# Moving a conditioned layer from blocks of 512 tokens behind a planned stage into that stage, sample by sample

## The chip, the cores and the metric

The kernel runs on one core of a Trainium2 chip. It uses five engines: TensorE (PE), which multiplies matrices; VectorE (DVE), ScalarE (ACT) and GpSimd (POOL), which work element by element; and SyncE (SP), which issues most of the transfers. Each engine runs its own list of instructions in order and waits on semaphores for the others. The metric is the device time of one launch, in microseconds (us), as the median of several runs. Everything is computed in float32.

## The reference

The input x holds 16 samples of 256 tokens with 256 features. Four residual steps follow one another. The change concerns the conditioned layer inside the last of them:

```python
# 1: x += attention0(cross_attention(x, side))                 16 heads of 16
# 2: x += fp4_feed_forward(x @ W[cat[b]] + b[cat[b]])          quantized in blocks of 16
# 3: x += segment_attention(reaction_diffusion(x, zX, zY, zR)) 16 heads of 64, segments of 128, 16 memory tokens
# 4:
h = gelu(x @ fc1_w.T + fc1_b)                   # 256 -> 1024, the erf form
shared = h @ fc2_w.T + fc2_b                    # 1024 -> 192
own = h @ experts_w[idx[b]].T + experts_b[idx[b]]   # 1024 -> 64, one of 16 experts per sample
y = concat(shared, own)                         # 256 features again
x += SCALE * (shared_expert(y) + sum(gate_e * expert_e(y) for the best 2 of 8 experts))
```

An expert of the mixture is 256 -> 1024, gelu (the tanh form), 1024 -> 256. The expert of the conditioned layer ("own") is chosen by the sample, those of the mixture by the token.

## The kernel before, in words

**Two parts.** `woven` (L329) does steps 1 to 3 for all samples; `mixture` (L1286) does step 4.

**The woven part** is written as 18 generators, one for each stage. stage_a, stage_m, stage_x and stage_e are step 1 (projections, scores, exponentials b_e, values and output projection); stage_y and stage_f are step 2 (the layer by category, then the quantized feed-forward with its tiles d_h, q_xn, q_big); stage_gate, stage_up and stage_down prepare its weights once; stage_d is the reaction-diffusion of step 3 (e_u, e_zT); stage_p, stage_k and stage_u make queries, keys and values of a group of four heads (weights wq and wv, rotated tiles f_t1q, f_t2q, f_t1k, f_t2k, which are moved into f_q and keys by transfers); stage_s, stage_g and stage_v do scores, exponentials (f_prob) and values with the output projection (f_pT, f_oT, wo, added to x); stage_c is described below; stage_fill gives PE idle products until the first sample is under way. There are 64 head groups in step 3, four for each sample.

**The planner.** `weave` (L201) merges the generators into one list of instructions for each engine, when the program is built. It keeps a model of when each engine is free and each tile is written and read (costs in L118 to L124). In each round it takes from every stage its next operation, works out at what time that could start, and issues the one that can start first; on a tie the stage that stands first in one list of stages, the same for all engines. An operation can have two choices of engine: `copy_` (L323) is a copy on ACT or DVE. Tiles live in rings of a fixed number of buffers; a new tile waits until the oldest buffer's readers are done. The order found is the order on the chip: an engine that waits for one operand lets nothing pass. Matmul results of the woven part go into PSUM tiles named `single` (four, one bank each) and `pair` (two, two banks each).

**Between the parts.** After step 1 of the last sample the memory of its tiles is given up, and `fetch_c` (L489) loads into it the first two samples of x from DRAM (`xd`, written by stage_v after step 3 of each sample) and the weights of the conditioned layer: fc1, fc2, wr (the router's weights), and two tiles own0 and own1, whose first 64 columns are shared and whose last 64 are a sample's own expert. `stage_c` (L518) then computes the first layer of block 0 (512 tokens, the hidden tile hT0) as the last stage of the woven part.

**The mixture part** is scheduled in program order. `conditioned` (L1594) loops over 8 blocks of 512 tokens: it loads own weights and later samples of x, transposes x (g_xT or xT), adds the shared expert's bias bs2 to x on POOL, computes 8 groups of 128 hidden columns of fc1 with a Gelu each, the 128 shared outputs with fc2, the 64 shared and 64 own outputs of each sample (yT), and the router's products (wr). `route` (L1463) chooses the experts and their ranks on DVE and sends each row of y to its two places in `ysort` by 8 indirect scatters per block from POOL (L1513). `plan_tiles` (L1521) then lays out the expert tiles, four shared blocks (`shared_block`, L1340, 512 tokens of the shared expert each) follow, then 35 expert tiles of 256 rows (`expert_tiles`, L1388), each of which loads its rows ys from `ysort` and its two weight matrices, then the other four shared blocks with `combine` (L1412), which gathers each token's two expert rows and stores the output.

The rule by which the planner chooses, and its costs:

```python
COSTS = {"DVE": (0.15, 0.00105), "ACT": (0.16, 0.00083), "POOL": (0.30, 0.0016)}
...
                found.append([start + (GAP if op.filler else 0.0), rank, c[1], w, c, start, part])
        if found:
            x = min(found, key=lambda x: x[:3])
            best = (x[:3], x[3], x[4], x[5])
```

Of the kernel before, what the change touches and what calls it, by code (L numbers as in the profile page):

```python
# [19 lines left out]
P = 128  # L20
# [42 lines left out]
def setup(ctx, tc, a, n_batch):  # L63
# [22 lines left out]

    k.xd = [dram.tile([S, D], F32, name=f"xd{b}") for b in range(n_batch)]
# [36 lines left out]
GAP = 0.6  # L124

# [9 lines left out]
def rows_of(op):  # L135

    if len(op.ins) < 2 or op.ins[0].shape[0] > 64:
        return None
    first, n = op.ins[0].start_partition() // 32, 1 + (op.ins[0].shape[0] > 32)
    return range(first, first + n), 0.15 + row_size(op.ins[1]) * 0.00178  # L140
# [17 lines left out]
class Unit:  # L158
# [5 lines left out]
    def __getattr__(self, fn):  # L164
        call = getattr(self.engine, fn)

        def make(*args, **kw):
            aps = [x for x in args if is_ap(x)] + [v for n, v in kw.items() if is_ap(v) and n not in ("out", "accum_out")]
            outs = [kw[n] for n in ("out", "accum_out") if n in kw and is_ap(kw[n])]
            if "out" not in kw:  # L170
                outs.insert(0, aps.pop(0))
            return Op([(self.name, self.cost(fn, outs, aps), lambda: call(*args, **kw))], outs, aps)  # L172

        return make
# [26 lines left out]
def weave(streams):  # L201
# [58 lines left out]
    waiting = [[s, None, None] for s in streams]  # L260
    while waiting:
        best, moved, found = None, False, []
        for rank, w in enumerate(waiting):
# [15 lines left out]
            for c in op.choices:  # L279
# [7 lines left out]
                found.append([start + (GAP if op.filler else 0.0), rank, c[1], w, c, start, part])  # L287
# [40 lines left out]

def woven(k):  # L329
    nc, tc = k.nc, k.tc  # L330
    with ExitStack() as ctx:
# [18 lines left out]
        g.x, g.io, g.done = {}, {}, {"J": 0, "T": 0, "K": 0, "X": 0, "S": 0, "VT": 0, "U": 0, "Y": 0, "H": 0, "W": 0, "D": 0, "Z": 0, "A": 0, "M": 0, "E": 0, "F": 0, "P": 0, "G": 0, "V": 0, "L": 0, "R": 0, "C": 0}  # L350
        with tc.manual_schedule():
            weave([stage_f(g), stage_a(g), stage_m(g), stage_x(g), stage_e(g), stage_v(g), stage_y(g), stage_d(g), stage_s(g), stage_g(g), stage_p(g), stage_k(g), stage_u(g), stage_gate(g), stage_up(g), stage_down(g), stage_c(g), stage_fill(g)])
# [50 lines left out]
def stage_a(g):  # L403
# [17 lines left out]
    for b in range(g.B):  # L421
# [3 lines left out]
        if b + 1 < g.B:  # L425
            yield lambda: b + 1 < g.done["L"] + 5
            yield from fetch_a(g, b + 1)
# [19 lines left out]
def stage_m(g):  # L447

    g.shifted = {}
# [39 lines left out]
def fetch_c(g):  # L489
# [3 lines left out]
    hT0 = k.h0.__enter__().tile([P, 8, 512], F32, name="hT0")  # L493
    k.c2 = k.tc.tile_pool(name="c2_w", bufs=1, side="right")
    w = k.c2.__enter__()
    k.early = {"hT0": hT0}

    def get(name, shape, src=None):
        k.early[name] = t = w.tile(shape, F32, name=name)
        if src is not None:  # L500
            yield g.sp.dma_start(out=t, in_=src)

    yield from get("x0", [P, 4, D])
    for b in range(2):
        yield g.sp.dma_start(out=k.early["x0"][:, 2 * b : 2 * b + 2, :], in_=k.xd[b].rearrange("(s p) d -> p s d", p=P))
    yield from get("fc1", [P, 2, FF1], a["fc1"])
    yield from get("fc1b", [P, 8], a["fc1b"])
    yield from get("fc2", [P, 8, P], a["fc2a"])
    yield from get("wr", [P, 2, P + NE])
    yield g.sp.dma_start(out=k.early["wr"][:, :, P:], in_=a["w_router"])  # L510
    for i in range(2):
        yield from get(f"own{i}", [P, 8, P])
        yield g.sp.dma_start(out=k.early[f"own{i}"][:, :, 0:64], in_=a["fc2c"])
    yield from get("xT0", [P, 2, 512])
# [3 lines left out]
def stage_c(g):  # L518


    yield lambda: g.done["C"] and g.done["G"] == 4 * g.B
    e = g.k.early
    x, xT = e["x0"], e["xT0"]
    for c in range(2):
        one = yield from single(g, x)
        pt = one.rearrange("p (s t) -> p s t", t=P)
        for s in range(4):
            yield g.pe.transpose(pt[:, s, :], x[:, s, c * P : (c + 1) * P], g.ident)
        yield copy_(g, xT[:, c, :], one)
        g.singles.append(one)  # L530
    for f in range(8):
        one = yield from single(g, xT)
        yield from mm_(g, one, [(e["fc1"][:, c, f * P : (f + 1) * P], xT[:, c, :]) for c in range(2)])
        yield g.act.activation(e["hT0"][:, f, :], one, AF.Gelu, bias=e["fc1b"][:, f : f + 1])
        g.singles.append(one)
# [37 lines left out]
def cross_attention(g, b):  # L573
# [17 lines left out]
    for st in range(2):  # L591
        yield g.dve.tensor_scalar(e[:, st, :], e[:, st, :], stat[:, 2 + st : 3 + st], None, ALU.mult)
# [49 lines left out]
def heads_scores(g, i):  # L642
# [19 lines left out]
    for st in (1, 0):  # L662
        n = (st + 1) * P
        four = yield from quad(g, t, kd)
# [6 lines left out]
        for jp, two in enumerate(four):  # L671
            e = g.a_.tile([P, 4, n], F32, name=f"b_e{st}", tag=f"b_e{st}", bufs=3)
# [82 lines left out]
def stage_y(g):  # L755
# [5 lines left out]
    for b in range(g.B):  # L761
        yield lambda b=b: g.done["A"] > b
        if b + 1 < g.B:
            yield from fetch_f(g, b + 1)
        g.yT[b] = yield from conditioned_rows(g, b)
# [3 lines left out]
def fetch_f(g, b):  # L769
    wc = g.f_.tile([P, 2, D], F32, name="wc", tag="wc", bufs=2)  # L770
    bc = g.f_.tile([P, D], F32, name="bc", tag="bc", bufs=2)
# [50 lines left out]
def scratch_l(g, wide, narrow):  # L822

    tags = dict(q_xn=wide[0], q_big=wide[1])
    shape = {"f_pT": [P, 4, P], "f_prob": [P, 2, 4, PM + P], "wq": [P, 2, 2, 2 * P], "f_v": [P, 2, 4 * DH1]}
    bufs = {"f_pT": 3, "f_prob": 2, "wq": 2, "f_v": 3}
# [54 lines left out]
def stage_down(g):  # L881

    g.downT = g.w.tile([P, 6, D], F32, name="downT")
    scratch = scratch_l(g, ("f_prob", "wq"), "down")
# [82 lines left out]
def stage_p(g):  # L967
# [34 lines left out]
    pmv = tile_l(g, [P, 2, 2, 2 * P], "wq", 2)  # L1002
    yield g.sp.dma_start(out=pmv, in_=a["pmv"].rearrange("p c (r w) -> p c r w", r=2))
    for c in range(2):
        wo = tile_l(g, [P, 4, D], "wq", 2)
        yield g.sp.dma_start(out=wo, in_=a["w_out1"][:, 4 * c : 4 * c + 4, :])
# [3 lines left out]
        for i in range(4):  # L1010
            yield g.pe.transpose(pt[:, i, :], pmv[:, c, i // 2, (i % 2) * P : (i % 2 + 1) * P], g.ident)
        yield copy_(g, pmvT, pt)
        g.singles.append(one)
        one = yield from single(g, pmvT, wo)
# [18 lines left out]
    g.wq, g.queries = {0: (yield from fetch_p(g, 0))}, {}  # L1033
    for i in range(4 * g.B):
        yield lambda: g.done["D"] > i // 4 and i < g.done["S"] + 2 and g.done["K"] >= i
        if i + 1 < 4 * g.B:
            g.wq[i + 1] = yield from fetch_p(g, (i + 1) % 4)
        q = g.queries[i] = tile_l(g, [P, 2, S], "f_q", 2)
        move = lambda half, a, src: g.sp.dma_start(out=q[half, a, :], in_=src)
        yield from turned4(g, g.zT[i // 4], g.wq[i][:, 0], "q", DH1**-0.5, move)  # L1040
# [3 lines left out]
def stage_k(g):  # L1044

    yield lambda: g.done["Z"]
    by_seg = lambda t: t.rearrange("p (s t) -> p s t", s=2)
    for i in range(4 * g.B):
        yield lambda: g.done["D"] > i // 4 and i < g.done["S"] + 4 and i in g.wq
        keys = g.keys[i % 4]  # L1050
        move = lambda half, a, src: g.sp.dma_start(out=keys[half, a, :, PM:], in_=by_seg(src))
        yield from turned4(g, g.zT[i // 4], g.wq[i][:, 1], "k", None, move)
# [51 lines left out]
def fetch_p(g, n):  # L1104

    wq = tile_l(g, [P, 2, 2, 2 * P], "wq", 2)
    for which in range(2):
        cols = slice((8 * which + 2 * n) * P, (8 * which + 2 * n + 2) * P)
        yield g.sp.dma_start(out=wq[:, which], in_=g.a["w_qk1"][:, :, cols])
    return wq  # L1110


def stage_u(g):
# [3 lines left out]
    for i in range(4 * g.B):  # L1117
# [3 lines left out]
        v, before = tile_l(g, [P, 2, 4 * DH1], "f_v", 3), wv  # L1121
        if i + 1 < 4 * g.B:
            wv = yield from fetch_u(g, (i + 1) % 4)
        zT = g.zT[i // 4]
        one = yield from single(g, before, zT)
        pv = one.rearrange("p (s d) -> p s d", s=2)
        for st in range(2):
            yield from mm_(g, pv[:, st, :], [(zT[:, c, st * P : (st + 1) * P], before[:, c, :]) for c in range(2)])
# [6 lines left out]
def fetch_u(g, n):  # L1135

    wv = tile_l(g, [P, 2, 4 * DH1], "wv", 2)
# [4 lines left out]
def turned4(g, zT, w, name, scale, move):  # L1142

    one = yield from single(g, w, zT)
    pq = one.rearrange("p (r t) -> p r t", r=2)
    for r in range(2):
        yield from mm_(g, pq[:, r, :], [(w[:, c, r * P : (r + 1) * P], zT[:, c, :]) for c in range(2)])
    t1, t2 = tile_l(g, [P, 2, S], f"f_t1{name}"), tile_l(g, [P, 2, S], f"f_t2{name}")
# [9 lines left out]
    for a in range(2):  # L1158
        for r in range(2):
            yield move(slice(r, P, 2), a, t1[64 * a : 64 * a + 64, r, :])  # L1160

# [4 lines left out]
def stage_s(g):  # L1166

    g.scored = {}
# [13 lines left out]

def stage_v(g):

    for i in range(4 * g.B):
# [4 lines left out]
        if n == 3:  # L1190
            yield g.sp.dma_start(out=g.k.xd[b].rearrange("(p s) d -> p s d", p=P), in_=g.x.pop(b))
# [27 lines left out]
def exponentials4(g, n, prob, stat):  # L1219

    wo = tile_l(g, [P, 2, D], "wo", 2)
    yield g.sp.dma_start(out=wo, in_=g.a["w_out1"][:, 2 * n : 2 * n + 2, :])
# [12 lines left out]
    return prob, g.pm, wo  # L1235


def values4(g, n, b, v, prob, pm, wo):
# [20 lines left out]
    oT = tile_l(g, [P, 2, S], "f_oT", 2)  # L1259
# [13 lines left out]
    for st in range(2):  # L1273
# [4 lines left out]
        yield from mm_(g, pp[:, st, :], pairs)  # L1278
    yield g.dve.tensor_tensor(g.x[b], g.x[b], pp, ALU.add)
# [6 lines left out]
def mixture(k, out):  # L1286
# [5 lines left out]
    with ExitStack() as ctx:  # L1292
# [4 lines left out]
        for b in range(2):  # L1297
# [3 lines left out]
        k.yT = keep.tile([P, 2, B * S], F32, name="yT")  # L1301
        k.b1 = keep.tile([P, NE + 1, 8], F32, name="b1")
        k.bs2 = keep.tile([P, D], F32, name="bs2")
        nc.sync.dma_start(out=k.b1, in_=a["b1"])
        nc.sync.dma_start(out=k.bs2, in_=a["b2"][NE : NE + 1].to_broadcast([P, D]))
        nc.vector.tensor_scalar(k.bs2, k.bs2, OUT_SCALE, None, ALU.mult)
        r = routing_state(k, keep)
        w1s = keep.tile([P, 2, FF1], F32, name="w1s")
        w2s = keep.tile([P, 8, D], F32, name="w2s")
# [464 lines left out]
```

## Time and profile before

| | us |
|---|---|
| median of 3 runs | 2705.15 (2704.03 to 2711.97) |
| profiled execution | 2715.88 |
| its span | 2714.1 |
| busy: PE, DVE, ACT, POOL | 2582.5, 1456.7, 1086.8, 987.0 |
| first product of the mixture part's experts | 2099.4 |

The profile is of one execution. A group of instructions is written as line, engine, operation, tile written, tile read, shapes and count; most operations of the woven part have line L172, where a helper records them, so tiles tell them apart. Busy shares of a slice are in tenths (9 is 90% or more). PEclk is the share of full speed that PE's clock was granted. A matmul of float32 over 128 rows and 256 columns shows as two records, and the weights of a matmul are loaded by PEld beside the one before. What stands in brackets after an instruction, or after `|` in a group, is the idle time of the engine just ahead of it and what ended it. A list of waits gives, for an instruction and what it waited for, the total in us, how many times, and the longest.

### The profile page before, as it was taken

To read this page: it belongs to the slowest core of one execution; us is meant where nothing else is said; L and a number is where in the kernel's file an instruction comes from. 1 tells how busy PE (TensorE), PEld (TensorE's weight loads), DVE (VectorE), ACT (ScalarE), POOL (GpSimd) and SP (SyncE) were. 2 spreads that over 40 slices of the span, in tenths; PEclk is the share of its full clock that TensorE was granted. 3 is DMA by queue.
4 is the path that set the end of the run, shared out by engine and by line. 5 is a ranking of instruction groups with operands and counts; after the bars stand their busy time and mean duration, and the time that the engine had idled before them with its cause. 6 is when DMAs were issued, how large, how long until landed. Compare 5 with 4: busy or idle time off the path is not lost. (4 is left out here: it accounts for less than half of the span.)

```text
span 2714.1 us, 39363 instructions
## 1 busy us (share of the span) xinstructions
PE 2582.5 (95%) x13521; PEld 1922.8 (71%) x13521; DVE 1456.7 (54%) x2815; ACT 1086.8 (40%) x3360; POOL 987.0 (36%) x1022
## 2 busy tenths in 40 slices
PE   8879899999899999899998999999999999999999
PEld 7757676776667776676776677665566888888866
DVE  7577877777777787677787665334330000000023
ACT  2343545554545554435563543333321232222321
POOL 5344545554444554445555443233320000000045
PEclk9989999999899999999999999999999999999999
DMA  4122234332234333134233236321120555555523
GB/s 130 55 75 70 84 113 130 105 114 66 80 107 145 100 105 111 49 123 129 79 114 94 76 112 186 94 89 47 47 95 10 181 192 197 199 189 188 198 86 109
DMA packets 249658, 303.60 MB, mean 112 GB/s; under 512 B 43120, under 2 KB 216432, under 8 KB 240112
## 3 DMA queue, kind: packets, MB, share of 16 engines
q1 hardware_dynamic: 243312, 284.26, 33.5%
q0 software_dynamic: 6144, 16.79, 2.0%
q8 instruction: 110, 1.80, 0.3%
q14 instruction: 92, 0.75, 0.1%
HBM read 206.85 MB, written 60.56 MB: 99 GB/s over the span
## 5 line engine op out<-in xcount | busy, mean ns | idle before, releaser
L1418 POOL DMA_INDIRECT got<-osort,pos_o x64 | 62.2, 972 | 624.5 <-SPq L1324 583.2
L172 POOL TENSOR_TENSOR b_e<-b_e,b_stat 128x512 f32<-128x512 f32 (+1 forms) x128 | 192.5, 1504 | 243.9 <-DVE b_stat L172 214.1
L1400 ACT ACTIVATE ehT<-bank,own_b 128x256 f32<-128x256 f32 x280 | 132.8, 474 | 348.9 <-PE bank L49 348.9
L172 PE MATMUL single<-e_zT,wq 128*128 128x256 f32 x1024 | 253.9, 391 | 3.1 <-DVE c_y L172 1.4
L49 PE MATMUL bank<-ysT,w 128*128 128x256 f32 x1120 | 247.5, 379 | 0.2 <-ACT ysT L105 0.2
L49 PE MATMUL bank<-w,ehT 128*128 128x256 f32 x1120 | 247.5, 379 | 0.0
L49 PEld LDWEIGHTS bank<-ysT,w 128*128 128x128 f32 x1120 | 212.7, 190 | 29.4 <-ACT ysT L105 0.5
L172 ACT ACTIVATE b_e<-b_e,b_stat 128x128 f32<-128x128 f32 (+1 forms) x512 | 225.8, 445 | 16.5 <-DVE b_stat L172 16.5
L49 PEld LDWEIGHTS bank<-w,ehT 128*128 128x128 f32 x1120 | 210.2, 190 | 27.2
L172 PEld LDWEIGHTS single<-e_zT,wq 128*128 128x128 f32 x1024 | 187.3, 192 | 41.4 <-issue 2.4
L172 ACT ACTIVATE f_prob<-f_prob,f_stat 128x144 f32<-128x144 f32 x512 | 206.0, 407 | 13.3 <-DVE f_stat L172 13.3
L172 PE MATMUL single<-wo,f_oT 128*128 128x256 f32 x512 | 136.1, 400 | 16.5 <-DVE f_oT L172 11.4
L1408 DVE TENSOR_TENSOR eo<-bank,eb 128x512 f32<-128x512 f32 x35 | 24.2, 692 | 234.4 <-PE bank L49 234.4
L172 ACT COPY b_pT<-single 128x512 f32<-128x512 f32 x140 | 80.5, 588 | 120.1 <-PE single L172 109.1
L172 DVE TENSOR_TENSOR x<-x,single 128x512 f32<-128x512 f32 (+1 forms) x112 | 68.0, 608 | 108.6 <-PE single L172 108.3
L172 PE MATMUL pair<-keys,f_q 64*128 64x144 f32 x1024 | 122.4, 327 | 4.1 <-DMA f_q<-f_t1q 2.2
L172 PE MATMUL single<-ident,b_e 128*128 128x128 f32 x768 | 117.6, 288 | 8.8 <-POOL b_e L172 5.8
L172 PE MATMUL single<-wv,e_zT 128*128 128x256 f32 x512 | 125.5, 388 | 0.0
L1367 DVE COPY own_b<-b1t 128x8 f32<-128x8 f32 x35 | 5.9, 175 | 222.4 <-ACT ehT L1400 222.3
L172 PEld LDWEIGHTS single<-wo,f_oT 128*128 128x128 f32 x512 | 98.0, 198 | 37.2 <-DVE f_oT L172 12.8
L1513 POOL DMA_INDIRECT ysort<-r_y,r_posi x64 | 62.6, 979 | 164.7 <-DMA ysort<-r_y,r_posi 108.0
L172 POOL TENSOR_TENSOR f_prob<-f_prob,f_stat 128x1024 f32<-128x1024 f32 x64 | 122.3, 1911 | 0.0
(309 smaller groups left out, 5445.3 us busy)
## 6 DMA issues: line engine op xcount, KB each, us to landing
w<-in_w SPq DMA_DIRECT2D x70, 1024.0 KB, 5.3
wq<-in_w_qk SPq DMA_DIRECT2D x128, 256.0 KB, 3.7
ysort<-zero SPq DMA_DIRECT2D x32, 1024.0 KB, 7.6
wv<-in_w_v SPq DMA_DIRECT2D x64, 256.0 KB, 3.4
f_q<-f_t1q SPq DMA_DIRECT2D x256, 64.0 KB, 2.0
keys<-f_t1k SPq DMA_DIRECT2D x256, 64.0 KB, 2.1
wo<-in_w_out SPq DMA_DIRECT2D x64, 256.0 KB, 3.6
ys<-ysort SPq DMA_DIRECT2D x35, 256.0 KB, 2.7
```

Of the source, the lines that this page charges most:

```text
L49: nc.tensor.matmul(out, lhsT, rhs, start=start and i == 0, stop=stop and i == last)
L172: return Op([(self.name, self.cost(fn, outs, aps), lambda: call(*args, **kw))], outs, aps)
L1367: nc.vector.tensor_copy(b1, r.b1t[:, t, :])
L1400: nc.scalar.activation(hT[:, f, :], ph, AF.Gelu_apprx_tanh, bias=b1[:, f : f + 1])
L1408: nc.vector.tensor_tensor(o, po, b2.unsqueeze(1).to_broadcast([P, 2, D]), ALU.add)
L1418: nc.gpsimd.indirect_dma_start(out=g, out_offset=None, in_=k.osort[:, :], in_offset=bass.IndirectOffsetOnAxis(ap=r.pos_o[:, i, t : t + 1], ...
L1513: nc.gpsimd.indirect_dma_start(out=k.ysort[:, :], out_offset=bass.IndirectOffsetOnAxis(ap=posi[:, i, t : t + 1], axis=0), in_=ys[t], in_of ...
```

## The change

1. *stage_b* takes the conditioned layer into the woven part, one sample at a time, once step 3 of that sample is done. Its weights are streamed: 16 pieces of 128 rows by 2 x 128 per sample through three buffers (`bw`), 20 transfers; the biases are added by ACT or DVE (`shifted_`), and one Gelu covers the sample's 128 x 2048 hidden values in place. y goes to DRAM (`yd`). stage_c is gone.
2. *The planner* has an order of stages for each engine (`ORDER`), makes DVE less welcome where an operation can go to ACT (`EASE`), counts a cost for a Gelu (`SWITCH`), and prefers by engine operations that read, or that don't read, PSUM (`BANK_LATER`). The scaling of a_e in step 1 may go to ACT (`scaled_`).
3. *Buffers* are halved to make room: wq is split into wq and wk with one buffer each; wv, wo, wc, bc and f_oT have one instead of two; the first half of b_e has two instead of three. The next weights are fetched right after the last use of the present ones. A sample's x is held until stage_b has read it.
4. *The mixture* loads y and x of all 16 samples at its start; for each block `routed` adds bs2, computes the router's products and routes. Shared blocks 0, 1 and 2 stand behind blocks 1, 3 and 5, and shared block 3 behind `plan_tiles`. Its weights (w1s, w2s, b1, bs2, wr) are loaded in `fetch_c`. A token's row in a tile is now (partition, half) instead of (half, partition), in x, in y's transposition and in the output.

The diff, cut to its core:

```diff
+AHEAD = 3
+SWITCH = 2.6
+EASE = 1.0
+ORDER = {
+    "PE": "f a m x e g y d b v s p k u gate up down fill",
+    "DVE": "f a m x d e s v b y g p gate u up k down fill",
+    "ACT": "f a m x e p v y b d g s k gate up u down fill",
+    "POOL": "a f m x y e v d s g p up k u gate down b fill",
+    "SP": "f a m x e v y d s g p k u gate up down b fill",
+}
+BANK_LATER = {"PE": None, "DVE": True, "ACT": False, "POOL": None, "SP": None}
...
-                found.append([start + (GAP if op.filler else 0.0), rank, c[1], w, c, start, part])
+                late = GAP if op.filler else 0.0
+                if c[0] == "DVE" and len(op.choices) > 1:
+                    late += EASE
+                late += 0.01 * (any(in_psum(x) for x in op.ins) == BANK_LATER[c[0]])
+                found.append([start + late, ranks[c[0]][w[0].__name__], c[1], w, c, start, part])
...
+def stage_b(g):
...
+    pieces = [(b, j) for b in range(g.B) for j in range(16)]
+    held, ahead = [], iter(pieces)
+
+    def fetch():
...
+        t = tile_l(g, [P, 2, P], "bw", AHEAD)
+        f = slice(2 * (j % 4), 2 * (j % 4) + 2)
+        if j < 8:
+            yield g.sp.dma_start(out=t, in_=a["fc1"][:, :, j * P : (j + 1) * P])
+        elif j < 12:
+            yield g.sp.dma_start(out=t, in_=a["fc2a"][:, f, :])
+        else:
...
+            yield g.sp.dma_start(out=t[:, :, 0:64], in_=a["fc2c"][:, f, :])
+            own = a["exp_w"][bass.ds(g.own, 1)].rearrange("e p f m -> p (e f) m")[:, f, :]
+            yield g.sp.dma_start(out=t[:, :, 64:128], in_=own)
+        held.append(t)
...
+    for b in range(g.B):
+        yield lambda: g.done["L"] > b
...
+        g.done["B"] = b + 1
+        hT = tile_l(g, [P, 8, S], "bh")
+        for f in range(8):
+            yield from fetch()
+            w = held.pop(0)
+            one = yield from single(g, w, xT)
+            yield from mm_(g, one[:, :S], [(w[:, c, :], xT[:, c, :]) for c in range(2)])
+            yield shifted_(g, hT[:, f, :], one[:, :S], small["fc1b"][:, f : f + 1])
+            g.singles.append(one)
+        yield g.act.activation(hT, hT, AF.Gelu)
...
+                for f in range(2):
+                    at = 2 * i + f
+                    yield g.pe.matmul(one[:, :S], w[:, f, :], hT[:, at, :], start=at == 0, stop=at == 7)
+            yield shifted_(g, y[:, half, :], one[:, :S], bias)
+            g.singles.append(one)
+        yield g.sp.dma_start(out=k.yd[b].rearrange("p (c s) -> p c s", c=2), in_=y)
...
-    wc = g.f_.tile([P, 2, D], F32, name="wc", tag="wc", bufs=2)
-    bc = g.f_.tile([P, D], F32, name="bc", tag="bc", bufs=2)
+    wc = g.f_.tile([P, 2, D], F32, name="wc", tag="wc")
+    bc = g.f_.tile([P, D], F32, name="bc", tag="bc")
...
-    wv = tile_l(g, [P, 2, 4 * DH1], "wv", 2)
+    wv = tile_l(g, [P, 2, 4 * DH1], "wv")
...
-    oT = tile_l(g, [P, 2, S], "f_oT", 2)
+    oT, wo = tile_l(g, [P, 2, S], "f_oT"), g.wo
...
-        conditioned(k, keep, r)
-        nc.sync.dma_start(out=w1s, in_=a["w1"][NE])
-        nc.sync.dma_start(out=w2s, in_=a["w2"][NE])
+        early = 4
+        with tc.tile_pool(name="c2_p2", bufs=2) as p2:
+            for blk in range(NT // 4):
+                k.stream = blk % 2
+                routed(k, p2, r, wr, blk)
+                if blk % 2 and blk // 2 < early - 1:
+                    shared_block(k, r, w1s, w2s, blk // 2)
         k.stream = 1
         plan_tiles(k, keep, r)
+        shared_block(k, r, w1s, w2s, early - 1)
...
 def load_x(k, b):
-    k.nc.sync.dma_start(out=k.xs[:, 2 * b : 2 * b + 2, :], in_=k.xd[b].rearrange("(s p) d -> p s d", p=P))
+    k.nc.sync.dma_start(out=k.yT[:, :, b * S : (b + 1) * S], in_=k.yd[b].rearrange("p (c s) -> p c s", c=2))
+    k.nc.sync.dma_start(out=k.xs[:, 2 * b : 2 * b + 2, :], in_=k.xd[b].rearrange("(p s) d -> p s d", p=P))
...
+def routed(k, p2, r, wr, blk):
+
+    nc = k.nc
+    x = k.xs[:, 4 * blk : 4 * blk + 4, :]
+    nc.gpsimd.tensor_tensor(x, x, k.bs2.unsqueeze(1).to_broadcast([P, 4, D]), ALU.add)
...
+    route(k, r, p2, logits, ys, 4 * blk, 4)
```

## The prediction

> **What bounds the kernel now.** I read the profile in this order: busy shares and slices, then the stretches by stage, then TensorE's list of waits, then single stretches of the timelines. TensorE (PE) is 95% busy, so it is the bound, and the question is where the other 5% lies and at which clock the 95% ran. First PE's row of slices and its granted clock:
>
> ```profile
> PE   8879899999899999899998999999999999999999
> PEclk9989999999899999999999999999999999999999
> ```
>
> Then the stretches (length, busy time of PE, PEld, DVE, ACT, POOL, granted clock, DMA share, GB/s). The woven part ends at about 1750, the first expert matmul is at 2099.4:
>
> ```profile
> 0.00:300.00 300.00, 261.91 (x1578) 200.11 (x1579) 216.09 (x385) 121.19 (x412) 142.46 (x158) 0.94 0.28 84
> 300.00:1000.00 700.00, 665.89 (x3884) 486.16 (x3882) 529.99 (x922) 348.48 (x1223) 351.59 (x354) 0.98 0.35 105
> 1000.00:1750.00 750.00, 701.14 (x4058) 512.58 (x4058) 523.14 (x902) 359.80 (x1259) 349.12 (x375) 0.96 0.34 102
> 1750.00:2100.00 350.00, 345.43 (x1256) 213.16 (x1255) 108.57 (x410) 92.63 (x137) 81.62 (x75) 1.00 0.21 68
> 2100.00:2714.00 614.00, 608.09 (x2755) 510.77 (x2753) 78.93 (x197) 164.73 (x329) 62.21 (x64) 1.00 0.51 170
> ```
>
> Length less PE busy is 38 + 34 + 49 = 121 us in the woven part and 10 behind it. (1 - clock) x length is 18 + 14 + 30 = 62 us, all woven. So 183 us are lost in the woven part: 56 in the first 300 us, 127 after. The mixture has no lost clock and 10 us of waits: what it takes is work. What ends the waits:
>
> ```profile
> PE single L172 <- DVE e_u L172: 12.7, 5, 7.4
> PE single L172 <- DVE f_oT L172: 11.7, 7, 4.4
> PE pair L172 <- DVE f_prob L172: 11.2, 3, 7.7
> PE single L172 <- POOL d_h L172: 10.9, 6, 4.5
> PE single L172 <- POOL f_prob L172: 8.6, 5, 4.9
> PE single L172 <- DVE a_e L172: 8.5, 5, 3.3
> ```
>
> (Total, times, longest.) They are few, long, and mostly behind VectorE (DVE). One of them, first on PE, then on DVE:
>
> ```profile
> 727.32 3.78 PE L172 MATMUL single<-wo,f_oT 128*128 128x256 f32 x8 [4.43 <-DVE f_oT L172]
> ```
> ```profile
> 722.47 1.54 DVE L172 TENSOR_SCALAR q_big<-q_big 128x704 int32<-128x704 int32 x1 [0.34 <-ACT q_big L172]
> 724.11 2.56 DVE L172 SCALAR_TENSOR_TENSOR q_xn<-q_big,q_xn 128x704 f32<-128x704 f32 x2
> 726.59 0.68 DVE L172 COPY f_oT<-single 128x512 f32<-128x512 f32 x1
> ```
>
> A copy that PE needs stood behind 4 us of quantization on DVE, while ScalarE (ACT) is 47% busy. The 8 matmuls after it took 3.78 us; the kernel's usual pace is 0.43 start to start for such a pair of records, so 1.7 to 1.9: the wait is paid about one and a half times.
>
> **The change, part by part**, against this execution (span 2714.1 us, 2715.9 with what lies around it, 10.7 above the median of the runs, 2705.15; I carry the difference over to the median).
>
> *Work moved into the woven part.* Per sample stage_b has 4 transposes (0.11 each) and 32 matmuls of 256 columns (0.43): 14.2 us; 16 samples 229. Block 0's first layer, 14.8 there now, goes. +214.
>
> *Mixture.* From 1750.6 to 2099.4 it is now 349 us, all PE: eight conditioned blocks of 31.3 and four shared blocks of 27.6. What stays is 110.5 of shared blocks, 14.8 for the router and about 6 of small products: 132 us. That would save 217. But something is late next. Each block has 8 indirect scatters, each waiting for the landing of the one before:
>
> ```profile
> 1781.04 0.96 POOL L1513 DMA_INDIRECT ysort<-r_y,r_posi  x1 [1.73 <-DMA ysort<-r_y,r_posi]
> 1783.71 0.96 POOL L1513 DMA_INDIRECT ysort<-r_y,r_posi  x1 [1.71 <-DMA ysort<-r_y,r_posi]
> 1786.39 0.96 POOL L1513 DMA_INDIRECT ysort<-r_y,r_posi  x1 [1.71 <-DMA ysort<-r_y,r_posi]
> 1789.56 0.96 POOL L1513 DMA_INDIRECT ysort<-r_y,r_posi  x1 [2.21 <-DMA ysort<-r_y,r_posi]
> ```
>
> That is 2.67 us each, with the irregular ones 22.3 per block (1778.06 to past 1797.65), hidden now under 31.3 us of PE. The scatters and their waits are unchanged, so eight blocks need 178 us, whatever PE does, and experts can't start before the last. Ahead of the first scatter: SP issues 32 loads (yT and xs) after the last store of y. The loads of xs now go out 13 in 8.5 us, so 21 us of issue; 8.4 MB at the 300 to 337 GB/s seen there take 26; landing some 3.5 more. In program order POOL has all eight additions of bs2 to xs (2.35 us each) ahead of the first scatter, the last of which needs the last load: first scatter at 32. Behind the last: ys and the first expert weights (5.3 to land, issue, transposes, copy) 9; breaks between blocks, since r_y has five buffers and later copies wait for scatters, 4. Sum 32 + 178 + 9 + 4 = 223, so PE is idle for some 90 us and the saving is 349 - 223 = 126, not 217. From the first expert matmul to the end nothing changes: 614.7.
>
> *Tail of the woven part.* The last sample's 16 pieces have no other work beside them in program order. Three buffers and 0.65 us per issue, 2.8 from issue to landing (ys 2.7), 0.88 of use: about 1.23 per piece, with one Gelu and its table load 27 us, of which 15 are counted above: +12. Bounds 0 and 25 (each piece alone: 16 x 2.8 less what is counted).
>
> *Added waits.* PE has 231 more semaphore waits (1643 for 1412, program order). Each costs between nothing (met early) and 0.09 (all 132 us of PE idle time over the present 1412): 0 to 22. I take 5, since the pieces are fetched two ahead.
>
> *SP.* 330 more issues x 0.65 = 215 us over some 1970. A piece's load waits for a buffer on SP's in-order queue, and f_q/keys moves (2.0 to land) and single-buffered wq, wk, wv, wo stand behind it; PE waits for those. Bounds: nothing, and 1 us for each of the 64 head groups, 64. I take nothing beyond the recovery below.
>
> *ACT and DVE.* Some 210 copies (0.69 on DVE, 0.59 on ACT) and 25 scalings leave DVE: 160 of its 1269 us. ACT gains 135, 160 shifts at about 0.4, 16 long Gelus at some 2.3 and 24 table loads: about 270 on 829, over a longer stage, 55%. Neither is a bound. The table load costs what these rows show, with no gap on either side:
>
> ```profile
> 1771.10 0.23 ACT L1471 ACTIVATE r_p<-r_p 128x32 f32<-128x32 f32 x1 [0.86 <-DVE r_p L1470]
> 1771.35 1.28 ACT L1637 ACT_TABLE_LOAD   x1
> 1772.64 1.27 ACT L1637 ACTIVATE hT<-bank,fc1b 128x512 f32<-128x512 f32 x2
> ```
>
> [...]
>
> *What the weaving gives back.* From the two programs' orders and the durations above I count the PE work that lies between a producer's input and its consumer, at the tightest places: e_u 2.16 to 4.31 us, d_h 2.72 to 5.09, a_e 0 to 1.53, f_prob 0 to 0.46, f_oT 0.22 to 0.52. Against the mean wait of each (2.5, 1.8, 1.7, 1.7, 1.7) the gain covers 85, 100, 90, 27 and 18%; weighted by the totals 64% of these five. The list is what was left over after a plan that had already filled what it foresaw, and f_prob's 7.7 us for a PSUM pair isn't touched, so I take 55% of the 127 after 300 us: 70. In the first 300 us no stage_b has anything to do; the copies alone give perhaps 15% of 56: 8. The lost clock is assumed to go with the waits. [...]
>
> **Sum:** 214 - 126 + 12 + 5 - 78 = **+27**: profiled 2743, median **2732 us**. Even is at 105 of the 183 recovered.
>
> **Rivals.**
> 1. *The woven losses nearly vanish* (faster). One mechanism: PE always has a loaded piece of stage_b ahead of a late consumer. It decides from 113 recovered; at 90% of 127 plus 35% of 56, 134: -29, 2676. For it: DVE's relief hits the very waits listed. Against: three buffers hold 2.6 us of work, waits reach 7.7.
> 2. *Pieces and moves queue on SP*: 20% of 127 recovered and 15 us of new waits: +95, 2800. For: single weight buffers. Against: DMA share 0.35.
> 3. *The scatters break up*: 8 us per block more than 22.3 put 64 on top of the forecast: +91, 2796; if instead the chain were hidden, the forecast falls by up to 91, to 2641. The spaced rows speak for neither.
> 4. *The change fills no gaps*, stage_b as good as appended: +105 or more, 2810. Program order has its pieces spread from the first seventh of PE's woven list to the end, against it.
>
> **Numbers.** Forecast with its neighbourhood (slower) 0.40, within 0.3% 0.12 (0.3% is what a measurement of this kernel can tell), rival 1 0.27, rival 2 0.11, rival 3 0.03 down and 0.04 up, rival 4 0.03. Faster 0.30, same 0.12, slower 0.58. The range 2660 to 2800 leaves out the better half of rival 3 down, part of rival 1 and what is beyond 2 and 4. The likeliest sign's own range is 2713 to 2775.
>
> **What would show it.** The woven part ending at 1751 + 214 + 17 - 78, about 1905; PE clock over 0.98 after 300 us; scatters 2.67 apart as PE's last cause, with 80 to 90 us of PE idle before the first expert; additions of bs2 ahead of the first scatter; 600 to 620 us from there to the end. Wrong would be: scatters closer together, a woven end under 1870 or over 1950.

## The result and the profile after

The changed kernel takes 2754.89 us (median of 4 runs, 2754.44 to 2760.15) for 2705.48 before: ratio 1.0179, interval 1.0166 to 1.0191. It is slower, by 49 us; the forecast was 27. The profiled execution took 2754.63, its span is 2752.7.

PE's slices and its granted clock, on the page of the changed kernel:

```profile
PE   8979999989999999999999999895685999999999
PEclk9989999999999999999999999998788999999999
```

The woven part has lost most of its low digits; a hole has come at slices 28 to 31, and the clock falls there (0.81 in the stretch from 1902.20), where it had been full (1.00 in the mixture before). The same in stretches; the cuts are the end of the woven part (1902.2) and the first expert matmul (2133.3):

```profile
0.00:300.00 300.00, 261.58 (x1575) 203.31 (x1576) 184.96 (x333) 141.66 (x441) 140.43 (x156) 0.92 0.28 84
300.00:1000.00 700.00, 686.53 (x4019) 513.93 (x4017) 446.17 (x768) 429.35 (x1334) 330.99 (x333) 1.00 0.40 115
1000.00:1750.00 750.00, 731.76 (x4210) 547.80 (x4209) 452.40 (x789) 447.71 (x1369) 330.32 (x341) 0.99 0.41 118
1750.00:1902.20 152.20, 137.77 (x786) 106.83 (x786) 47.14 (x79) 74.15 (x208) 37.01 (x42) 0.96 0.42 118
1902.20:2133.30 231.10, 149.07 (x582) 100.11 (x582) 79.08 (x375) 42.84 (x68) 82.75 (x87) 0.81 0.24 83
2133.30:2752.70 619.40, 613.22 (x2760) 513.95 (x2760) 79.51 (x198) 164.77 (x329) 62.31 (x64) 0.99 0.52 173
```

By the reckoning used ahead (length less PE busy, and length times missing clock) the woven part behind 300 us now loses 46 + 14 = 60 us, where it lost 127. The mixture part up to the experts has 82 us without PE work. VectorE's load between 300 and 1750 fell from 1053 to 899 us. PE's waits:

```profile
PE bank L49 <- DVE r_sel L1587: 21.5, 3, 10.8
PE bank L49 <- issue: 21.4, 1, 21.4
PE single L185 <- POOL d_h L185: 14.6, 4, 6.4
PE bank L100 <- DMA ys<-ysort: 12.2, 1, 12.2
PE single L185 <- POOL c_y L185: 9.6, 2, 9.4
PE single L185 <- DVE e_u L185: 8.7, 3, 7.3
```

f_oT, f_prob and a_e, behind VectorE, are gone from the top. Three of the first four lines are of the mixture (bank): PE there waits for the routing (the 21.4 us put down to "issue" end at 1935.17 with the first product that reads r_sel) and, at the end, for the rows that the scatters have laid down. GpSimd, at the start and the end of the chain:

```profile
1930.33 2.34 POOL L1690 TENSOR_TENSOR xs<-xs,bs 128x1024 f32<-128x1024 f32 x1 [0.36 <-DMA xs<-xd]
1938.99 1.25 POOL L1605 DMA_INDIRECT ysort<-r_y,r_posi  x1 [6.32 <-DVE r_tmp L1598]
1941.98 0.96 POOL L1605 DMA_INDIRECT ysort<-r_y,r_posi  x1 [1.73 <-DMA ysort<-r_y,r_posi]
...
2123.54 0.96 POOL L1605 DMA_INDIRECT ysort<-r_y,r_posi  x1 [1.70 <-DMA ysort<-r_y,r_posi]
```

The first scatter goes 36.8 us after the woven part. The last starts 184.6 us after it, 2.93 apart on the mean, and the first expert matmul follows 9.7 after that, behind two waits of PE:

```profile
2128.90 1.11 PE L100 MATMUL bank<-ident,ys 128*128 128x128 f32 x4 [12.21 <-DMA ys<-ysort]
2133.26 9.64 PE L49 MATMUL bank<-ysT,w 128*128 128x256 f32 x32 [3.25 <-DMA w<-in_w]
```

What held the first scatter is seen on VectorE:

```profile
1921.85 0.42 DVE L1573 TENSOR_TENSOR r_eq<-r_p 128x256 f32<-128x256 f32 x1
1930.43 2.86 DVE L1574 TENSOR_TENSOR r_eq<-r_eq,tri 128x256 f32<-128x256 f32 x2 [8.16 <-DMA tri<-in_tri]
```

`tri` is a constant of 8 x 8 for the routing; its load stands on SP behind the 32 loads of y and x (issued at 1925.4). The additions of bs2 were done at 1932.7, so they were the second bar, not the first.

### The profile page after: what moved, and what is told of

Read it like the earlier page. It is cut to its first block, busy times and chain, and to the rows that moved or that the text cites. A ratio compares the mean times of both kernels' runs of the same rounds, so it can differ in the third digit from the quotient of the medians.

```text
span 2752.7 us, 40948 instructions
## 1 busy us (share of the span) xinstructions
PE 2579.9 (94%) x13927; PEld 1985.9 (72%) x13927; DVE 1289.3 (47%) x2541; ACT 1300.5 (47%) x3746; POOL 983.8 (36%) x1022
## 5 line engine op out<-in xcount | busy, mean ns | idle before, releaser
L185 ACT COPY b_pT<-single 128x512 f32<-128x512 f32 x191 | 111.2, 590 | 122.4 <-PE single L185 122.0
L185 POOL TENSOR_TENSOR f_t1q<-f_t1q,f_t2q 128x256 f32<-128x256 f32 x128 | 93.0, 744 | 179.3 <-DVE f_t2q L185 135.2
L185 PE MATMUL single<-bh,bw 128*128 128x256 f32 x512 | 135.7, 390 | 5.8 <-ACT bh L185 3.8
L185 PE MATMUL single<-bx,bw 128*128 128x256 f32 x512 | 133.7, 385 | 6.3 <-DMA bw<-in_fc 5.6
L185 PE MATMUL single<-wo,f_oT 128*128 128x256 f32 x512 | 130.5, 388 | 3.1 <-ACT f_oT L185 3.1
L185 PE MATMUL single<-e_zT,wq 128*128 128x256 f32 x512 | 128.3, 395 | 0.0
L49 PE MATMUL bank<-yT,w1s 128*128 128x512 f32 x256 | 122.4, 638 | 5.7 <-DVE r_tmp L1582 2.5
L185 PE MATMUL single<-e_zT,wk 128*128 128x256 f32 x512 | 126.0, 389 | 0.0
L185 DVE TENSOR_TENSOR f_prob<-pair,mask 128x576 f32<-128x576 f32 x128 | 95.3, 745 | 63.6 <-PE pair L185 62.7
```

What stands on the lines that cost most here:

```text
L49: nc.tensor.matmul(out, lhsT, rhs, start=start and i == 0, stop=stop and i == last)
L185: return Op([(self.name, cost, lambda: call(*args, **kw))], outs, aps)
```

## The experiments

Two theories on the mixture: the start and the chain of scatters set when the experts begin; or PE and the routing do, and the chain runs beside them. Two on the woven part: the copies moved to ScalarE won the time back; or the matmuls of stage_b did, by filling holes.

### Half the scatters

```diff
     for t in range(n):
-        for i in range(TOPK):
+        for i in range(1):
             nc.gpsimd.indirect_dma_start(
```

> The changed kernel with the second of each token's two scatters left out (32 scatters for 64; half of the rows that the experts then read are the zeros laid there before, so the output differs; the same tiles are run). Theory: the chain of scatters (184.6 us from first to last, 2.93 each) sets when the first expert may start. 32 fewer take 94 us off the chain, and PE's own work and the start (37 us) come next: 60 to 80 us less, 2675 to 2695. Rival: PE waits for the routing on VectorE (r_sel) and the loads, the chain runs beside it: at most 15 us less, 2740 or more.

2716.12 us, 39 less than the changed kernel: between the two. The woven part ended at 1903.0, the first expert matmul came at 2093.3, so the stretch is 190.3 instead of 231.1. PE at its end:

```profile
2061.39 16.96 PE L49 MATMUL bank<-yT,w1s 128*128 128x512 f32 x32
2078.19 13.98 PE L49 MATMUL bank<-w2s,hT 128*128 128x256 f32 x64
2092.00 1.04 PE L100 MATMUL bank<-ident,ys 128*128 128x128 f32 x8
2093.28 6.96 PE L49 MATMUL bank<-ysT,w 128*128 128x256 f32 x31 [0.24 <-ACT ysT L106]
```

Now PE ends the stretch: no gap ahead of the experts, and the last scatter is 18 us earlier. So the chain is the bound of the changed kernel, but by 41 us only. Behind it stands PE with the routing: the start, 146 us of matmuls at a lower clock (0.85 over the stretch; 16.96 for 32 records that took 13.90 in the kernel before, at a clock of 1.00) and the waits for the routing, for which the scatters themselves now stood still three times (10.7 to 19.0 us).

### The start, and what stands among the scatters

The small table first, then y, then x; the additions of bs2 made to depend on the last block's gates:

```diff
+        r = routing_state(k, keep)
         for b in range(B):
-            load_x(k, b)
+            load_y(k, b)
+        for b in range(B):
+            load_x(k, b)
...
+        last = r.gate[:, 0, NT - 1 : NT].to_broadcast([P, D])
+        nc.vector.scalar_tensor_tensor(late, last, 0.0, k.bs2, ALU.mult, ALU.add)
+        for blk in range(NT // 4):
+            x = k.xs[:, 4 * blk : 4 * blk + 4, :]
+            nc.gpsimd.tensor_tensor(x, x, late.unsqueeze(1).to_broadcast([P, 4, D]), ALU.add)
```

> The changed kernel with the routing's small table loaded ahead of y and x, all of y ahead of x, and the additions of bs2 to x behind most of the scatters on GpSimd. Theory (chain sets the start of the experts): the first scatter comes 15 to 20 us after the woven part instead of 37, all else follows, less 3 to 5 for additions that now lie between the last scatters: 10 to 20 less, 2735 to 2745. Rival (PE and VectorE set it): within 5 of 2755.

2760.62 us: nothing gained. The first scatter did come 21 us after the woven part, but the chain grew from 184.6 to 202.7, and the trace says where, on GpSimd:

```profile
2082.79 0.96 POOL L1616 DMA_INDIRECT ysort<-r_y,r_posi  x1 [1.70 <-DMA ysort<-r_y,r_posi]
2083.78 6.95 POOL L1414 TENSOR_TENSOR xs<-xs,bs_late 128x1024 f32<-128x1024 f32 x3
2090.89 0.99 POOL L1616 DMA_INDIRECT ysort<-r_y,r_posi  x1 [0.16 <-issue]
```

Two or three additions at a time stood between scatters. My edit had moved them into the chain. So I put them behind an expert tile (only the line that makes `late` moves, to the eleventh tile, reading its output eo instead of the gates):

> The early start again (small table, then y, then x loaded), with the eight additions of bs2 put off until an expert tile (the eleventh) has been computed, so that none lies among the scatters as in the run before, where they took 22 us of the chain between 2083 and 2106. Theory (the experts start when start and chain of scatters are done): the first scatter 21 us after the woven part as there, the rest as in the changed kernel: 12 to 17 less than it, 2738 to 2743. Rival (PE and the routing set the end of this stretch, since with half the scatters it still took 190 us): at most 5 less.

2750.16 us (2742.32 to 2754.64), 5 less, which as a time is the rival's. But the stretch shrank as the theory has it, 231.1 to 216.9; in the profiled execution the woven part, whose instructions are the same, ended at 1916.2 instead of 1902.2, which hid it. The chain theory holds for the stretch; the medians show a third of it. Then the other two things that the trace names, the buffers and the idle PE:

```diff
-        y = p2.tile([P, 2, P], F32, name="r_y", tag="r_y", bufs=5)
+        y = p2.tile([P, 2, P], F32, name="r_y", tag="r_y", bufs=16)
...
-        early = 4
+        early = 5
...
-                if blk % 2 and blk // 2 < early - 1:
-                    shared_block(k, r, w1s, w2s, blk // 2)
+                if blk in AFTER:
+                    shared_block(k, r, w1s, w2s, AFTER.index(blk))
```

(`AFTER` is (1, 3, 4, 5); the gathers of the end are spread over three blocks.)

> The same, with 16 buffers instead of 5 for the rows that are scattered, and five shared blocks instead of four ahead of the experts (behind blocks 1, 3, 4, 5 and the plan), three instead of four behind them. Theory: without the waits for buffers the scatters come every 2.67 us (13 us less), and the shared block moves into PE time that is idle beside them (27.6 at the end, less what the gathers then need: 64 at 1.25 us are 80, three blocks 83): 2698 to 2715. Rival (PE is the bound of the stretch): the moved block is paid there, 2725 or more.

2738.77 us: as a time the rival's side, but not for the rival's reason. The stretch is 225.2, 8 longer than without the moved block of 27.6, and the part behind the first expert matmul 605.1, 14 shorter, since the gathers there don't follow. The chain, which now takes 192.9, still ends the stretch:

```profile
1941.22 0.96 POOL L1618 DMA_INDIRECT ysort<-r_y,r_posi  x1 [1.70 <-DMA ysort<-r_y,r_posi]
1944.39 0.96 POOL L1618 DMA_INDIRECT ysort<-r_y,r_posi  x1 [2.20 <-DMA ysort<-r_y,r_posi]
2078.51 0.96 POOL L1618 DMA_INDIRECT ysort<-r_y,r_posi  x1 [8.89 <-DVE cnt L1637]
2127.88 1.11 PE L100 MATMUL bank<-ident,ys 128*128 128x128 f32 x4 [20.23 <-DMA ys<-ysort]
```

PE waits 20.2 us for the last rows. The chain did not tighten to 2.67, for two reasons. No scatter waits for a row's buffer any more, but every fourth still comes 3.17 after the one before; so it does in the kernel before and in the changed one, where six further such steps are all that the buffers can have cost in this way. And the moved block (2037 to 2065 on PE) stands ahead of the routing products of the seventh block, whose first scatter came 9.9 after the one before. Four repairs of the mixture together give 16 us, a third of the loss.

### The planner without stage_b

The kernel before with the new planner: ORDER (with c in the place of b), EASE, SWITCH, BANK_LATER, the costs of small matmuls (`rows_of`) and `scaled_`.

> The kernel before with the planner of the changed one (order by engine, EASE, SWITCH, BANK_LATER, costs of small matmuls, a_e scaling on either engine; stage_c in the place of stage_b in each list) and nothing else. The woven part lost 126 us after its first 300 before and 59 in the changed kernel. Theory one: the copies moved to ScalarE did that. Then this kernel gets it too, and its mixture still hides the scatters: 45 to 65 less than before, 2640 to 2660. Theory two: the matmuls of stage_b filled the holes. Then at most 15 less, 2690 or more.

2666.17 us, ratio to before 0.9848 (0.9831 to 0.9864). The woven part ends at 1702.1, and the mixture still takes 348 us with no gap. That is 6 us short of theory one's range and far from theory two's: 41 us of the recovery need no stage_b. The complement, the changed kernel under the old rule:

```diff
-EASE = 1.0
+EASE = 0.0
+ORDER = dict.fromkeys(("PE", "DVE", "ACT", "POOL", "SP"), "f a m x e v y d s g p k u gate up down b fill")
+BANK_LATER = dict.fromkeys(ORDER)
```

> The changed kernel with the old rule of choice in its planner: one order for all engines, EASE 0, no preference for or against PSUM. stage_b stays. Theory one (copies did it): the holes come back, 40 to 65 slower than the changed kernel, 2795 to 2820. Theory two (stage_b fills the holes whatever engine copies): within 15 of it, 2740 to 2770.

2799.75 us, 45 slower than the changed kernel: its woven part ends at 1953.8, its mixture takes 229.4. So far theory one. Then I took the planner apart, in the kernel before:

> The kernel before with the copies made less welcome on VectorE (EASE 1.0), the a_e scaling on either engine and the costs of the new planner, but one order of stages for all engines and no preference for or against PSUM. If the choice of engine for copies is what gave 41 us in the run with both, this has most of it: 2665 to 2680. If the order by engine gave it: 2695 or more.

2659.54 us (ratio 0.9827, 0.9810 to 0.9843).

> The kernel before with the orders by engine, the PSUM preference, the a_e scaling on either engine and the new costs, but EASE 0: copies go where they can start first, as before. If the choice of engine gave the 41 us: 2690 to 2705. If the order gave it: 2665 to 2680.

2669.25 us (0.9860, 0.9843 to 0.9876). Both halves do nearly all of it alone, so "it is the copies" was too simple: VectorE has 2815 instructions in the kernel before, 2574 with EASE, and 2765 with the orders, which move few copies. Was it what the two had in common?

> The kernel before with only what the last two runs had in common: the a_e scaling on either engine, the costs of small matmuls and of a Gelu; one order, EASE 0. Choice of engine alone gave 49 us, orders alone 39, both 42. If the common part does it: 2665 to 2680, and neither EASE nor the orders matter much. If each of the two opens the same holes by itself: 2695 to 2710.

2718.71 us, 12 slower than before and beyond both ranges: no.

> The kernel before with EASE 1.0 and nothing else of the change: one order, old costs, the a_e scaling on VectorE. If moving copies to ScalarE is enough: 2655 to 2675. If the common part is what worked: 2690 or more.

2656.05 us, ratio 0.9807 (0.9791 to 0.9824), with this edit alone:

```diff
-                found.append([start + (GAP if op.filler else 0.0), rank, c[1], w, c, start, part])
+                late = GAP if op.filler else 0.0
+                if c[0] == "DVE" and len(op.choices) > 1:
+                    late += EASE
+                found.append([start + late, ranks[c[0]][w[0].__name__], c[1], w, c, start, part])
```

(with `ranks` the old order for every engine). This beats both kernels. Its stretches:

```profile
300.00:1000.00 700.00, 671.44 (x3997) 492.02 (x3995) 498.39 (x863) 404.73 (x1361) 367.27 (x370) 1.00 0.35 106
1000.00:1695.50 695.50, 658.48 (x3924) 482.77 (x3922) 466.61 (x797) 382.38 (x1285) 332.89 (x358) 0.99 0.36 108
1695.50:2043.50 348.00, 343.74 (x1253) 212.47 (x1252) 107.63 (x407) 92.72 (x137) 81.46 (x73) 1.00 0.20 66
```

Behind 300 us the woven part loses 66 us of idle time and 7 of clock, where it lost 83 and 44: by this reckoning most of what came back is clock. So EASE alone is enough; what the orders repair without it isn't shown, and no run tells how much any other order of the same work would have given. Last, whether stage_b fits that plan (the changed kernel, one order, EASE 1.0):

> The changed kernel with one order for all engines and no PSUM preference, but EASE 1.0. Theory: stage_b and the new mixture cost the same under any plan (+92 under the old rule, 2799.75 for 2707.66; +89 under the new one, 2754.89 for 2666.17), so 2659.5 + 90: 2743 to 2757. Rival: stage_b needs the orders by engine to fit in: 2770 or more.

2798.12 us: the rival. The woven part ends at 1953.1, as under the old rule; EASE gives nothing there. PE's waits in that kernel between 300 and 1953 us:

```profile
PE single L179 <- ACT bh L179: 14.8, 8, 3.8
PE single L179 <- POOL d_h L179: 10.7, 5, 7.3
PE single L179 <- DVE bx L179: 10.0, 3, 4.2
PE single L179 <- POOL f_prob L179: 8.7, 2, 7.6
PE single L179 <- DVE e_u L179: 7.2, 5, 3.6
PE single L179 <- ACT bx L179: 6.5, 3, 2.9
```

PE waits 31 us for stage_b's own results (bh, bx), where the changed kernel waits 4 to 5. In the one order stage_b stands last on ScalarE and VectorE, in the orders by engine ninth on both. That this is what the orders repair is argued from the waits, and one trace speaks against it as the whole of it: under the old rule, in the same order, PE waits only 7 us for bh and bx, and the woven part ends no earlier. No run moved stage_b alone in the order.

Ends of the woven part (us): each row is one planner, each column one way of doing the conditioned layer; "stage_b" includes the halved buffers, which no run took apart from it. Each figure is from one profile.

| planner | as before | stage_b | difference |
|---|---|---|---|
| old rule (with the common part) | 1752.1 | 1953.8 | 201.7 |
| EASE only (with it) | 1693.6 | 1953.1 | 259.5 |
| orders and EASE | 1702.1 | 1902.2 | 200.1 |

### Before, once more

> The kernel before once more, for its profile. The first profiled execution was 10.7 us above the median of the runs. Theory: the length of the woven part differs from execution to execution (the same program in four variants of the changed kernel ended between 1902 and 1916): here 1740 to 1751, with all else within 1 us of the first profile. Rival: the profile itself costs it, then again 1750.

2707.91 us. Its woven part ended at 1743.6 instead of 1750.6; the stretch to the experts took 347.9, the rest 614.7. The first profile had caught an execution with a longer woven part: here the clock from 1000 to its end was 0.97 instead of 0.96, and PE's busy time 2572.4 instead of 2582.5. So the same program's woven part differs by 7 us here, and by up to 14 in the five profiles of the changed one's. Here it is PE's busy time that differs (1629.5 and 1620.0 us up to that end), not its idle time (121.1 and 123.6).

## Why the prediction was right, and where its sum was short

Slower was right, and the mechanism was: woven work paid in full, mixture saving cut by the chain of scatters, part of the losses won back. By terms, against the second profile of before (2706.2, close to the median), the difference is 46.5:

- *Woven part:* +158.6 measured, +153 forecast (214 + 12 + 5 - 78). The forecast end, 1905, was met by 1902.2, though the second profile puts the base 7 lower.
- *What the weaving gives back:* the 78 was nearly right as a sum, by luck, since it was wrong in its parts. Idle time and lost clock of the woven part together fell from 178 us to 122, so 56 came back, net of the tail and the added waits, where the forecast has 78 - 12 - 5 = 61. stage_b costs 201.7 under the old rule; if the forecast's 231 for the work is right, 29 came from its filling, 52 from the orders and EASE, and the common part cost 9 (1743.6 to 1752.1, little more than the executions differ). I had laid all of it to more PE work between producers and consumers. Most of it was to be had without stage_b. The work itself is 16 x 14.2 = 227, not 229.
- *Lost clock:* of the 44 us behind 300 us, 14 remain; I had taken a return of 55%.
- *Tail:* from the last sample's transposes (1876.98) to the end it took 25 us, for 27.
- *In the first 300 us* I took 8 off 56; 62 were lost, so nothing came back there.
- *Mixture to the experts:* -116.8 for -126. The start was 36.8 instead of 32, and I named the additions of bs2 where the table `tri` was the bar. The scatters took 184.6 from first to last, for 178 and 4 of breaks: the 22.3 per block already held a step of 3.17 at every fourth scatter; six further ones, four of them behind a row's copy (r_y), and breaks of up to 3.6 made up the rest. The end was 9.7 instead of 9.
- *The rest:* +4.7 where I had "nothing changes". The first expert product, behind waits of 12.2 and 3.3 us, took 9.6 us instead of 7.2, at a granted clock of 0.74 instead of 1.00: the lower clock was the term I had left out in the mixture as a whole (0.81 over the stretch ahead of it). The other 2 us aren't traced.
- *If the chain were hidden*, I took 91 off. Half the scatters took 39: I had put PE's own 132 us in its place and forgotten the start, the routing's waits and the clock, with which the stretch still took 190.
- *Carrying the difference over to the median* was worth 8 to 10 us: the one profile of before was a long execution.
- *SP's queue* was taken at nothing and cost little: PE waited 7.4 us for the pieces (bw, 5.6 of it from fc1) and 4.4 for wv.
- *Table loads:* in the changed kernel the load ahead of a Gelu is 1.28 us (1888.40) and the Gelu of 128 x 2048 starts at 1889.70, 0.02 behind it, and takes 1.91, for some 2.3.

## What to carry to other kernels

Work moved out of a stage is worth only what that stage has above its next bound: here 217 us of matmuls left a stretch whose scatters, hidden until then, take 185 and start late. And of a change that moves work and tunes the plan at once, each half should be timed alone: the smallest part, one constant in the choice of engine, was worth 51 us, and the kernel with the whole change is 99 slower than the one with that constant alone.

## What the runs showed of the hardware

- Indirect scatters that waited for one another went every 2.67 us (0.96 on GpSimd and 1.71 until the one before has landed), and every fourth 3.17 (0.96 and 2.21), also with 16 buffers, where no row's copy had to wait. What the fourth waits for isn't shown.
- The same instructions of the woven part took 7 to 14 us more or less in different executions. Between the two profiles of before PE's idle time hardly moved (121.1 and 123.6); its busy time did (1629.5 and 1620.0), with the granted clock (0.96 and 0.97 behind 1000 us).
- PE's granted clock was 0.81 between 1902 and 2133 of the changed kernel, where PE was busy 65% of the time, 0.85 at 77% with half the scatters, and 1.00 at 99% in the same part of the kernel before (1750.6 to 2099.4). 32 records of 512 columns took up to 16.98 us in the changed kernel instead of 13.90 in the one before. In the woven part of before the granted clock was 0.50 in 22 stretches of 3.4 to 13.7 us, more than PE had long waits there (five of 4.4 to 7.8 us, all others 3.3 or less). What brings the clock down isn't shown.
